# A routed feed-forward kernel: four PSUM banks for transposed rows, two for gate and up, and one piece for a unit's transposes

## The chip, the cores and the metric

The kernel runs on one core of a Trainium2 chip. Five engines work side by side, each on its own queue in order: TensorE (PE) multiplies, VectorE (DVE) and ScalarE (ACT) do elementwise work, GpSimd (POOL) issues the indirect transfers (gathers and scatters), SyncE (SP) the plain ones. PE reads from SBUF and writes to PSUM, which has eight banks of 128 x 512 fp32. The metric is the device time of one launch in microseconds. Before the change it is 3706.62 us, the median of three runs (3705.96 to 3707.15).

## The reference, cut to what matters

Tokens are 8 x 1024 = 8192 rows of 512 channels. A conditioning layer gives y; a feed-forward layer with one shared expert and 64 routed ones, eight per token, is added to x:

```python
y = clip(einsum(x * styles, weight) * dcoefs + bias, -256, 256)      # conditioning
shared = silu(y @ sh_gate_w) * (y @ sh_up_w) @ sh_down_w            # hidden 1024
topk_idx, w = route(y)                                              # 8 of 64 experts per row
g = ragged_dot(sorted_y, gate_w, group_sizes)                       # 512 -> 256, per expert
u = ragged_dot(sorted_y, up_w, group_sizes)
o = ragged_dot(silu(g) * u, down_w, group_sizes)                    # 256 -> 512
out = x + shared + zeros.at[tok].add(o * w)                         # scatter-add
```

All products are taken to fp32 accuracy: each operand is split into a high part (fp32r) and a low part, and a product is three matmuls, high x high, low x high, high x low.

## The kernel before, in words

The kernel has three stages. The conditioning runs first and writes y to memory, by rows. The shared expert follows, while the routing is worked out beside it. From about 1296 us on only the routed part is left, which is what the change touches.

The routed part works in blocks of 128 rows that go to one expert, and units of 1, 2 or 4 blocks that share one load of the expert's weights: 20 units of one block (NH), 16 of two (NP), 120 of four (NF), 532 blocks in all, with the kinds spread evenly over the sequence; unit 0 has four blocks. Further groups of units exist for other routings, behind conditions that are not met here.

For a unit, in order:

- SP loads the weights (`load`, L542): gate and up as `wg`, down as `wd`. ACT rounds them to the high parts `gh`, `dh` (`w_hi`, L560), DVE subtracts for the low parts `gl`, `dl` (`w_lo`).
- POOL gathers each block's 128 rows of y into one of 12 buffers `xg` (`gather`, L545).
- PE turns each block with four 128 x 128 transposes into one PSUM bank `pt` (`turn_x`, L549); ACT and DVE read that bank for `xh` (L552) and `xl`.
- PE makes gate and up in PSUM banks `pg`. A unit of four blocks has four products of 12 matmuls with 512 columns (`part`, L572): gate and up for the first half of the hidden channels, then for the second. ACT takes silu of the gate bank into `hf` (L716), DVE multiplies with the up bank (`mu`, L719), and `hh`, `hl` are split from `hf`. Units of two blocks do the same once, with 256 columns. A unit of one block is computed with rows on the partitions: gate and up share one bank (`half`, L581, 12 matmuls), and after silu and `mu` (L672, L673) PE turns the hidden rows (`turn_h`, L586) into the next `pg` bank, from which `hh` and `hl` are read.
- PE makes one down product per block, six matmuls with 512 columns into one of two banks `po` (`down_c`, L592); ACT weighs it into one of six buffers `oc` (L596); POOL scatters it with add into `out` (`scatter`, L599). The scatters of a unit wait for those of the unit before.

Before the change PSUM is split into two banks `pt`, four `pg` and two `po`. A block may be turned when the block two before it has been read; a gate or up result may start when the one four before it has been read.

The order of the work on each engine is fixed when the program is built. `plan` writes down a task for every step: engine, estimated duration, a lag until others see the result, a due time, and the tasks it comes after. `arrange` plays these estimates through: an engine that is free takes, of its ready tasks, the one due first. The order that comes out is the order of the queues; on the chip each instruction waits for what it really needs. Due times are set per unit from `due`, the running sum of PE's estimated work: `TURN` says how far ahead of it the transposes are due (first entry, and a step per block), `DOWN` how far behind the hidden rows the down products are. The last four units have due times of their own for the down products. Unit 0's transposes are emitted by hand during the end of the shared part.

The lines that decide the reuse of the banks:

```python
def pt_of(g):
    return pt[g % 2 if pt[1] is not None else 0]
...
add((i, "turn", s), "PE", 0.34, 0.45, t0, lambda u=u, s=s, g=g: turn_x(u, s, g), T[i, "gather", s], get(("xlo", g - 2)))
...
def wait_bank(b):
    return [bank[b - 4]] if b >= 4 else []
```

Of the kernel before, what the change touches and what calls it, by code (L numbers as in the profile page):

```python
# [15 lines left out]
ALU = mybir.AluOpType  # L16
# [50 lines left out]
def body(ctx, tc, xT, x, condT, wT, vecs, affT, rwT, ebias, wexp, shgu, shdn, cst, out):  # L67
# [32 lines left out]
    rctx, cctx = ExitStack(), ExitStack()  # L100
    FIRST = dict(xg=8, wg=2, wd=2, gh=1, gl=1, xh=1, xl=1)
    RX, ROC, RXG = 2, 6, 12
    sw = rctx.enter_context(tc.tile_pool(name="sw", bufs=1, side="right", reuse_waits="tile"))
    rp = rctx.enter_context(tc.tile_pool(name="rp", bufs=1, side="right", reuse_waits="tile"))
    yp = dctx.enter_context(tc.tile_pool(name="yp", bufs=6, reuse_waits="tile"))
# [384 lines left out]
    gh, gl, dh, dl, hh, hl = ([None] * 2 for _ in range(6))  # L490
    xh, xl = [None] * RX, [None] * RX
    hf, oc, xg = [None] * 3, [None] * ROC, [None] * RXG
    pt, po, pg = [None] * 2, [None] * 2, [None] * 4
    kinds = [
        (wg, [P, 2048], F32, "wg"), (wd, [P, 1024], F32, "wd"), (xg, [P, C], F32R, "xg"),
        (gh, [P, 2048], F32R, "gh"), (gl, [P, 2048], F32R, "gl"), (xh, [P, KC, QT], F32R, "xh"), (xl, [P, KC, QT], F32R, "xl"),
# [29 lines left out]
        return i_  # L526

    def pt_of(g):
        return pt[g % 2 if pt[1] is not None else 0]


    def load(u, a):
# [25 lines left out]
    def w_hi(u, c):  # L558
        a, sl = (gh, slice(c * 1024, (c + 1) * 1024)) if c < 2 else (dh, slice(0, 1024))
        S.copy(a[u.q][:, sl], (wg, wg, wd)[c][u.kind][:, sl])  # L560

    def w_lo(u, c):
        h_, l_, sl = (gh, gl, slice(c * 1024, (c + 1) * 1024)) if c < 2 else (dh, dl, slice(0, 1024))
        sub(l_[u.q][:, sl], (wg, wg, wd)[c][u.kind][:, sl], h_[u.q][:, sl].bitcast(F32))
# [18 lines left out]

    def turn_h(u, f, b):
        for m in range(2):
            PE.transpose(pg[b % 4][:, m * P:(m + 1) * P], hf[f % 3][:, m * P:(m + 1) * P], ident)  # L586

    def down_c(u, s, d):
        n = 0
# [23 lines left out]

    DOWN = {1: (-8.2, 1.0), 2: (6.6, 5.1), 4: (6.6, 5.1)}
    TURN = {1: (9.9, 1.0), 2: (13.2, 1.9), 4: (18.0, -1.3)}

    def plan(units):

# [2 lines left out]
        def add(key, eng, dur, lag, due, do, *after):  # L623
            t = Task(eng, dur, lag, due, do, after)
            T[key] = t
            tasks.append(t)
            return t
# [7 lines left out]
        for n, u in enumerate(units):  # L635
# [6 lines left out]
                before = [T[lw, x, 2 if a else c] for x in ("wh", "wl") for c in ((0, 1) if a == 0 else (2,))] if lw is not None else []  # L642
                add((i, "load", a), "SP", 0.1, 12.0 if a == 0 else 8.0, due - 22 + 4 * a, lambda u=u, a=a: load(u, a), *before)
            for c in range(2):
                add((i, "wh", c), "ACT", 1.08, 0.15, due - 8.3 + 2.2 * c, lambda u=u, c=c: w_hi(u, c), T[i, "load", 0], get((i - 2, "gu")))
                add((i, "wl", c), "DVE", 1.22, 0.15, due - 7.2 + 2.2 * c, lambda u=u, c=c: w_lo(u, c), T[i, "wh", c], get((i - 2, "gu")))
            xlo = []
            for s in range(u.nb):
                g = ng
                ng += 1  # L650
                t0 = due - TURN[u.nb][0] - (u.nb - 1 - s) * TURN[u.nb][1]
                gts[g] = (i, "turn", s)
                add((i, "gather", s), "POOL", 1.3, 4.5, t0 - 9, lambda u=u, s=s, g=g: gather(u, s, g), get(gts.get(g - RXG)))
                add((i, "turn", s), "PE", 0.34, 0.45, t0, lambda u=u, s=s, g=g: turn_x(u, s, g), T[i, "gather", s], get(("xlo", g - 2)))
                add((i, "xh", s), "ACT", 0.62, 0.15, t0 + 0.6, lambda u=u, s=s, g=g: x_hi(u, s, g), T[i, "turn", s], get((i - RX, "gu")))
                xlo.append(add((i, "xl", s), "DVE", 0.69, 0.15, t0 + 1.3, lambda u=u, s=s, g=g: x_lo(u, s, g), T[i, "xh", s], get((i - RX, "gu"))))
                T["xlo", g] = xlo[-1]
# [1 line left out]
            hq = [T[i - 2, "down", s] for s in range(units[n - 2].nb)] if n >= 2 else []  # L659

            def wait_bank(b):
                return [bank[b - 4]] if b >= 4 else []

            def wait_hf(f):
                return hfs.get(f - 3, [])
# [1 line left out]
            if u.nb == 1:  # L667
                b, f = nb_, nf_
                nb_, nf_ = nb_ + 2, nf_ + 1
                g0 = add((i, "gu0"), "PE", 1.37, 0.1, due, lambda u=u, b=b: half(u, 0, pg[b % 4]), *xlo, T[i, "wl", 0], T[i, "wl", 1], *wait_bank(b))  # L670
                g1 = add((i, "gu"), "PE", 1.37, 0.5, due + 1.37, lambda u=u, b=b: half(u, 1, pg[b % 4]), g0)
                si = add((i, "si"), "ACT", 0.37, 0.15, due + 3.0, lambda b=b, f=f: S.activation(hf[f % 3][:, :256], pg[b % 4][:, :256], AF.Silu), g1, *wait_hf(f))  # L672
                mu = add((i, "mu"), "DVE", 0.40, 0.15, due + 3.4, lambda b=b, f=f: V.tensor_tensor(hf[f % 3][:, :256], hf[f % 3][:, :256], pg[b % 4][:, 256:], ALU.mult), si)  # L673
                bank[b] = mu
                th = add((i, "th"), "PE", 0.3, 0.5, due + 3.9, lambda u=u, f=f, b=b: turn_h(u, f, b + 1), mu, *wait_bank(b + 1))
                o_ = lambda a, u=u: a[u.q][:, :, :P]
                p_ = lambda b=b: pg[(b + 1) % 4][:, :256].rearrange("p (m s) -> p m s", m=2)
                h_ = add((i, "hh"), "ACT", 0.37, 0.15, due + 4.6, lambda o_=o_, p_=p_: S.copy(o_(hh), p_()), th, *hq)
                l_ = add((i, "hl"), "DVE", 0.40, 0.15, due + 5.0, lambda o_=o_, p_=p_: sub(o_(hl), p_(), o_(hh).bitcast(F32)), h_, *hq)
                bank[b + 1] = l_  # L680
                hfs[f] = [th]
                lo = [l_]
                ddue = due + 5.6
            elif u.nb == 2:
                b, f = nb_, nf_
                nb_, nf_ = nb_ + 2, nf_ + 1
                prev = []
                for o in range(2):
                    for m in range(2):
                        p = add((i, "gu") if o and m else (i, "gu", o, m), "PE", 1.45, 0.5, due + 1.45 * (2 * o + m),  # L690
                                lambda u=u, o=o, m=m, b=b: part(u, o, m, pg[(b + o) % 4][:, m * 256:(m + 1) * 256]),
                                *xlo, T[i, "wl", o], *(wait_bank(b + o) if m == 0 else []), *prev)
                        prev = [p]
                    if o == 0:
                        si = add((i, "si"), "ACT", 0.61, 0.15, due + 3.2, lambda b=b, f=f: S.activation(hf[f % 3], pg[b % 4], AF.Silu), p, *wait_hf(f))
                        bank[b] = si
                mu = add((i, "mu"), "DVE", 0.69, 0.15, due + 6.1, lambda b=b, f=f: V.tensor_tensor(hf[f % 3], hf[f % 3], pg[(b + 1) % 4], ALU.mult), si, p)
                bank[b + 1] = mu
                o_ = lambda a, u=u: a[u.q][:, :, :256]
                p_ = lambda f=f: hf[f % 3].rearrange("p (m s) -> p m s", m=2)  # L700
                h_ = add((i, "hh"), "ACT", 0.61, 0.15, due + 6.9, lambda o_=o_, p_=p_: S.copy(o_(hh), p_()), mu, *hq)
                l_ = add((i, "hl"), "DVE", 0.69, 0.15, due + 7.6, lambda o_=o_, p_=p_: sub(o_(hl), p_(), o_(hh).bitcast(F32)), h_, *hq)
                hfs[f] = [l_]
                lo = [l_]
                ddue = due + 8.5
            else:
                prev = []
                for m in range(2):
                    b, f = nb_, nf_
                    nb_, nf_ = nb_ + 2, nf_ + 1  # L710
                    for o in range(2):
                        p = add((i, "gu") if o and m else (i, "gu", o, m), "PE", 2.73, 0.5, due + 2.73 * (2 * m + o),
                                lambda u=u, o=o, m=m, b=b: part(u, o, m, pg[(b + o) % 4]), *xlo, T[i, "wl", o], *wait_bank(b + o), *prev)
                        prev = [p]
                        if o == 0:
                            si = add((i, "si", m), "ACT", 0.61, 0.15, due + 5.46 * m + 3.1, lambda b=b, f=f: S.activation(hf[f % 3], pg[b % 4], AF.Silu), p, *wait_hf(f))  # L716
                            bank[b] = si
                    t0 = due + 5.46 * m + 5.8
                    mu = add((i, "mu", m), "DVE", 0.69, 0.15, t0, lambda b=b, f=f: V.tensor_tensor(hf[f % 3], hf[f % 3], pg[(b + 1) % 4], ALU.mult), si, p)  # L719
                    bank[b + 1] = mu  # L720
                    h_ = add((i, "hh", m), "ACT", 0.61, 0.15, t0 + 0.8, lambda u=u, m=m, f=f: S.copy(hh[u.q][:, m], hf[f % 3]), mu, *hq)  # L721
                    l_ = add((i, "hl", m), "DVE", 0.69, 0.15, t0 + 1.5, lambda u=u, m=m, f=f: sub(hl[u.q][:, m], hf[f % 3], hh[u.q][:, m].bitcast(F32)), h_, *hq)
                    hfs[f] = [l_]
                    lo.append(l_)
                ddue = t0 + 2.5
            for c in (2,):
                add((i, "wh", c), "ACT", 1.08, 0.15, ddue + 3.8, lambda u=u, c=c: w_hi(u, c), T[i, "load", 1], *hq)
                add((i, "wl", c), "DVE", 1.22, 0.15, ddue + 5.0, lambda u=u, c=c: w_lo(u, c), T[i, "wh", c], *hq)

            first, step_ = (2.0, 3.0) if len(units) - n <= 4 else DOWN[u.nb]  # L730
            chain = [T[units[n - 1].i, "out", s] for s in range(units[n - 1].nb)] if n else []
# [521 lines left out]
```

## Time and profile before

| | |
|---|---|
| median of three runs | 3706.62 us (3705.96 to 3707.15) |
| the profiled execution | 3707.15 us, span from first to last instruction 3705.4 us |
| granted PE clock | 0.998 |
| busy | PE 99%, POOL 56%, DVE 54%, ACT 47% |
| transposes of gathered rows (L549) | 2128 matmuls, 226.8 us busy |
| gate and up (L572) | 6528 matmuls, 2486 us busy |
| down (L592) | 3192 matmuls, 1263 us busy |
| evacuation of `pt` | xh 532 x 587 ns on ACT, xl 532 x 687 ns on DVE |

An engine's busy time counts overlapping instructions once. A PE matmul of 512 columns is shown with about 390 ns, but the next one starts before it has ended, so the distance between two starts, not the duration, is what a matmul costs. A line of the timeline reads: start in us from the beginning of the span, duration, engine, line of the program, operation, output and inputs, shapes, and how many in a row (xN); in brackets the idle time before it and what ended that. A line of the waits reads: who waited, for whom, us in total, times, longest.

### The profile page before, as it was taken

What the parts mean: (1) busy time and instruction counts of PE and PEld (TensorE: products, weight loads), DVE (VectorE), ACT (ScalarE), POOL (GpSimd) and SP (SyncE); (2) the same over time, 40 slices, a digit from 0 to 9 for tenths busy, and PEclk for the clock granted to TensorE, in tenths of its full rate; (3) what the DMA queues carried; (4) which work ended last, traced back from release to release, by engine and by line L of the source; (5) the groups of instructions that cost most, each with busy time, mean ns of one, the idle gap of its engine ahead of it and who ended that gap; (6) DMA issues with size and microseconds to landing.
All of it is one profiled execution on the core that took longest, in us unless ns stands there. A gap on an engine that the chain in (4) does not pass through costs nothing.

```text
span 3705.4 us, 49590 instructions
## 1 busy us (share of the span) xinstructions
PE 3679.9 (99%) x17819; PEld 3051.6 (82%) x17819; DVE 2009.1 (54%) x3196; ACT 1730.0 (47%) x2676; POOL 2092.1 (56%) x1597
## 2 busy tenths in 40 slices
PE   9999999999999999999999999999999999999997
PEld 7888888888888888888888888888888888888886
DVE  7765666666653355555455555455545555555553
ACT  6652111111111255555555555555556555555554
POOL 0002666666665155666666656665656656666663
PEclk9999999999999999999999999999999999999999
DMA  8852213122121377777777777777777777777664
GB/s 264 268 152 67 58 41 64 35 50 55 41 63 43 103 181 156 148 142 161 151 139 162 161 193 157 175 172 193 144 171 148 167 148 181 162 155 133 114 118 65
DMA packets 238739, 491.23 MB, mean 133 GB/s; under 512 B 43074, under 2 KB 75858, under 8 KB 230803
## 3 DMA queue, kind: packets, MB, share of 16 engines
q0 software_dynamic: 135840, 280.28, 40.4%
q1 hardware_dynamic: 101651, 206.63, 18.5%
q8 instruction: 142, 2.33, 0.3%
q10 hardware_dynamic: 992, 1.06, 0.1%
q14 instruction: 114, 0.93, 0.1%
HBM read 443.20 MB, written 195.63 MB: 172 GB/s over the span
## 4 chain that ended last, share of the span: by engine, by line
PE 98%; DVE 1%; DMA 0%; ACT 0%; POOL 0%; issue 0%; SPq 0%; POOLq 0%; DVEq 0%; ACTq 0%
PE pg L572 38%; PE po L592 20%; PE gu L124 19%; PE po L1091 9%; PE pt L549 4%; PE py L321 4%; PE pg L581 1%; PE plt L353 1%; DMA xr<-in_xT 0%; PE psm L376 0%; DMA wr<-in_wT 0%; DVE yl L72 0%; POOL out L599 0%; PE pg L586 0%; PE ps L1012 0%
## 5 line engine op out<-in xcount | busy, mean ns | idle before, releaser
L599 POOL DMA_INDIRECT out<-oc,tokw x532 | 918.8, 1727 | 664.3 <-DMA out<-oc,tokw 171.3
L572 PE MATMUL pg<-xh,gh 128*128 128x512 f32 (+1 forms) x2176 | 839.5, 386 | 0.0
L572 PE MATMUL pg<-xh,gl 128*128 128x512 f32 (+1 forms) x2176 | 824.3, 379 | 0.0
L572 PE MATMUL pg<-xl,gh 128*128 128x512 f32 (+1 forms) x2176 | 822.4, 378 | 0.0
L1061 POOL DMA_INDIRECT tab_d<-tokw,ad x512 | 567.0, 1107 | 443.2 <-DVE h L136 162.2
L545 POOL DMA_INDIRECT xg<-y_d,tokw x532 | 592.8, 1114 | 321.4 <-PE pt L549 131.0
L72 DVE TENSOR_TENSOR xl<-pt,xh 128x512 fp32r<-128x512 f32 x532 | 352.7, 687 | 406.4 <-ACT xh L552 405.6
L596 ACT ACTIVATE oc<-po,tokw 128x512 f32<-128x512 f32 x532 | 367.2, 690 | 315.6 <-PE po L592 276.0
L572 PEld LDWEIGHTS pg<-xh,gl 128*128 128x128 f32 x2176 | 409.3, 188 | 78.2
L572 PEld LDWEIGHTS pg<-xl,gh 128*128 128x128 f32 x2176 | 410.0, 188 | 71.6
L572 PEld LDWEIGHTS pg<-xh,gh 128*128 128x128 f32 x2176 | 409.1, 188 | 70.8
L719 DVE TENSOR_TENSOR hf<-hf,pg 128x512 f32<-128x512 f32 x240 | 165.0, 687 | 488.4 <-PE pg L572 488.4
L592 PE MATMUL po<-dh,hh 128*128 128x512 f32 x1064 | 428.4, 403 | 0.8 <-ACT hh L721 0.8
L592 PE MATMUL po<-dh,hl 128*128 128x512 f32 x1064 | 418.5, 393 | 0.0
L592 PE MATMUL po<-dl,hh 128*128 128x512 f32 x1064 | 415.7, 391 | 0.0
L72 DVE TENSOR_TENSOR gl<-wg,gh 128x1024 fp32r<-128x1024 f32 x312 | 376.3, 1222 | 52.0 <-ACT gh L560 51.6
L124 PE MATMUL gu<-yl,guh 128*128 128x512 f32 x1024 | 400.8, 391 | 0.2 <-DVE yl L72 0.2
L124 PE MATMUL gu<-yh,guh 128*128 128x512 f32 x1024 | 400.0, 391 | 0.1
L124 PE MATMUL gu<-yh,gul 128*128 128x512 f32 x1024 | 398.5, 389 | 0.0
L552 ACT CAST xh<-pt 128x512 fp32r<-128x512 f32 x532 | 296.7, 587 | 189.5 <-PE pt L549 134.7
L560 ACT CAST gh<-wg 128x1024 fp32r<-128x1024 f32 x312 | 324.0, 1048 | 27.4 <-PE pg L572 27.4
L716 ACT ACTIVATE hf<-pg 128x512 f32<-128x512 f32 x240 | 143.8, 599 | 295.0 <-PE pg L572 290.1
(246 smaller groups left out, 5200.0 us busy)
## 6 DMA issues: line engine op xcount, KB each, us to landing
wg<-in_wexp SPq DMA_DIRECT2D x156, 1024.0 KB
wd<-in_wexp SPq DMA_DIRECT2D x156, 512.0 KB
y_d<-yt SPq DMA_DIRECT2D x64, 256.0 KB
xn<-in_x SPq DMA_DIRECT2D x64, 256.0 KB
out<-xn SPq DMA_DIRECT2D x64, 256.0 KB
xr<-in_xT SPq DMA_DIRECT2D x60, 256.0 KB
yT_d<-yf SPq DMA_DIRECT2D x60, 256.0 KB
yr<-yT_d SPq DMA_DIRECT2D x60, 256.0 KB
```

What stands on the lines that cost most here:

```text
L72: V.tensor_tensor(o, a, b, ALU.subtract)
L124: i_ = PE.matmul(p_, lhsT=w_[:, q * KC + k], rhs=y_[k], start=n == 0, stop=n == 3 * KC - 1)
L545: queued(GP.indirect_dma_start(xg[g % RXG].bitcast(F32), None, y_d, IOA(slot_tok[:, u.block + s:u.block + s + 1], 0)))
L552: S.copy(xh[u.xq][:, :, s * P:(s + 1) * P], pt_of(g).bitcast(F32))
L560: S.copy(a[u.q][:, sl], (wg, wg, wd)[c][u.kind][:, sl])
L572: PE.matmul(out, lhsT=w_[u.q][:, c:c + P], rhs=x_[u.xq][:, k, :w], start=n == 0, stop=n == 3 * KC - 1)
L592: PE.matmul(po[d % 2], lhsT=h_[u.q][:, k, s * P:(s + 1) * P], rhs=w_[u.q][:, k * C:(k + 1) * C], start=n == 0, stop=n == 5)
L596: S.mul(oc[d % ROC], po[d % 2], slot_w[:, u.block + s:u.block + s + 1])
L599: i_ = queued(GP.indirect_dma_start(out, IOA(slot_tok[:, u.block + s:u.block + s + 1], 0), oc[d % ROC], None, compute_op=ALU.add))
L719: mu = add((i, "mu", m), "DVE", 0.69, 0.15, t0, lambda b=b, f=f: V.tensor_tensor(hf[f % 3], hf[f % 3], pg[(b + 1) % 4], ALU.mult), si, p)
L1061: i_ = GP.indirect_dma_start(places, IOA(ad, 0), tw, None)
L1091: PE.matmul(acc[j][s], lhsT=h_[:, ts], rhs=w_[c], start=c == 0 and n == 0, stop=c == HC - 1 and n == 2)
```

## The change

PSUM's split becomes four banks `pt`, two `pg`, two `po`. A block may be turned when the block four before it has been read, and a gate or up result may start when the one two before it has been read. Every unit of two or four blocks, except unit 0, gets one PE task that turns all its blocks in a row; it comes after all gathers of the unit, and after the reading of the `pt` banks that it fills. Due times of the transposes, of the down products and of the weights' casts are new numbers. Nothing changes in what is computed.

```diff
+    RPT, RPG = 4, 2
...
-    pt, po, pg = [None] * 2, [None] * 2, [None] * 4
+    pt, po, pg = [None] * RPT, [None] * 2, [None] * RPG
...
-        return pt[g % 2 if pt[1] is not None else 0]
+        return pt[g % RPT if pt[1] is not None else 0]
...
-    DOWN = {1: (-8.2, 1.0), 2: (6.6, 5.1), 4: (6.6, 5.1)}
-    TURN = {1: (9.9, 1.0), 2: (13.2, 1.9), 4: (18.0, -1.3)}
+    DOWN = {1: (-7.2, 1.0), 2: (8.4, 5.1), 4: (8.7, 6.2)}
+    TURN = {1: (12.2, 1.0), 2: (8.9, 1.3), 4: (17.7, -0.9)}
...
-                add((i, "wh", c), "ACT", 1.08, 0.15, due - 8.3 + 2.2 * c, lambda u=u, c=c: w_hi(u, c), T[i, "load", 0], get((i - 2, "gu")))
-                add((i, "wl", c), "DVE", 1.22, 0.15, due - 7.2 + 2.2 * c, lambda u=u, c=c: w_lo(u, c), T[i, "wh", c], get((i - 2, "gu")))
+                add((i, "wh", c), "ACT", 1.08, 0.15, due - 11.1 + 2.2 * c, lambda u=u, c=c: w_hi(u, c), T[i, "load", 0], get((i - 2, "gu")))
+                add((i, "wl", c), "DVE", 1.22, 0.15, due - 10.0 + 2.2 * c, lambda u=u, c=c: w_lo(u, c), T[i, "wh", c], get((i - 2, "gu")))
...
-                add((i, "gather", s), "POOL", 1.3, 4.5, t0 - 9, lambda u=u, s=s, g=g: gather(u, s, g), get(gts.get(g - RXG)))
-                add((i, "turn", s), "PE", 0.34, 0.45, t0, lambda u=u, s=s, g=g: turn_x(u, s, g), T[i, "gather", s], get(("xlo", g - 2)))
+                if not (n and u.nb > 1 and s):
+                    add((i, "gather", s), "POOL", 1.3, 4.5, t0 - 9, lambda u=u, s=s, g=g: gather(u, s, g), get(gts.get(g - RXG)))
+
+                if n == 0 or u.nb == 1:
+                    add((i, "turn", s), "PE", 0.34, 0.45, t0, lambda u=u, s=s, g=g: turn_x(u, s, g), T[i, "gather", s], get(("xlo", g - RPT)))
+                elif s == 0:
+                    for q in range(1, u.nb):
+                        gts[g + q] = (i, "turn", q)
+                        add((i, "gather", q), "POOL", 1.3, 4.5, t0 - 9 + q, lambda u=u, q=q, g=g: gather(u, q, g + q), get(gts.get(g + q - RXG)))
+                    all_ = lambda u=u, g=g: [turn_x(u, q, g + q) for q in range(u.nb)]
+                    t = add((i, "turn", 0), "PE", 0.34 * u.nb, 0.45, t0, all_, *[T[i, "gather", q] for q in range(u.nb)], *[get(("xlo", g + q - RPT)) for q in range(u.nb)])
+                    for q in range(1, u.nb):
+                        T[i, "turn", q] = t
...
             def wait_bank(b):
-                return [bank[b - 4]] if b >= 4 else []
+                return [bank[b - RPG]] if b >= RPG else []
...
-                add((i, "wh", c), "ACT", 1.08, 0.15, ddue + 3.8, lambda u=u, c=c: w_hi(u, c), T[i, "load", 1], *hq)
-                add((i, "wl", c), "DVE", 1.22, 0.15, ddue + 5.0, lambda u=u, c=c: w_lo(u, c), T[i, "wh", c], *hq)
+                add((i, "wh", c), "ACT", 1.08, 0.15, ddue + 4.7, lambda u=u, c=c: w_hi(u, c), T[i, "load", 1], *hq)
+                add((i, "wl", c), "DVE", 1.22, 0.15, ddue + 5.9, lambda u=u, c=c: w_lo(u, c), T[i, "wh", c], *hq)
```

Everywhere else `pg[b % 4]` becomes `pg[b % RPG]`.

More of the change, by code (lines that the diff above doesn't have):

```diff
@@ L585, in turn_h @@
         for m in range(2):
-            PE.transpose(pg[b % 4][:, m * P:(m + 1) * P], hf[f % 3][:, m * P:(m + 1) * P], ident)
+            PE.transpose(pg[b % RPG][:, m * P:(m + 1) * P], hf[f % 3][:, m * P:(m + 1) * P], ident)
     def down_c(u, s, d):
@@ L669, in plan @@
                 nb_, nf_ = nb_ + 2, nf_ + 1
[L670 to L673, printed above, removed]
+                g0 = add((i, "gu0"), "PE", 1.37, 0.1, due, lambda u=u, b=b: half(u, 0, pg[b % RPG]), *xlo, T[i, "wl", 0], T[i, "wl", 1], *wait_bank(b))
+                g1 = add((i, "gu"), "PE", 1.37, 0.5, due + 1.37, lambda u=u, b=b: half(u, 1, pg[b % RPG]), g0)
+                si = add((i, "si"), "ACT", 0.37, 0.15, due + 3.0, lambda b=b, f=f: S.activation(hf[f % 3][:, :256], pg[b % RPG][:, :256], AF.Silu), g1, *wait_hf(f))
+                mu = add((i, "mu"), "DVE", 0.40, 0.15, due + 3.4, lambda b=b, f=f: V.tensor_tensor(hf[f % 3][:, :256], hf[f % 3][:, :256], pg[b % RPG][:, 256:], ALU.mult), si)
                 bank[b] = mu
@@ L676, in plan @@
                 o_ = lambda a, u=u: a[u.q][:, :, :P]
-                p_ = lambda b=b: pg[(b + 1) % 4][:, :256].rearrange("p (m s) -> p m s", m=2)
+                p_ = lambda b=b: pg[(b + 1) % RPG][:, :256].rearrange("p (m s) -> p m s", m=2)
                 h_ = add((i, "hh"), "ACT", 0.37, 0.15, due + 4.6, lambda o_=o_, p_=p_: S.copy(o_(hh), p_()), th, *hq)
@@ L690, in plan @@
                         p = add((i, "gu") if o and m else (i, "gu", o, m), "PE", 1.45, 0.5, due + 1.45 * (2 * o + m),
-                                lambda u=u, o=o, m=m, b=b: part(u, o, m, pg[(b + o) % 4][:, m * 256:(m + 1) * 256]),
+                                lambda u=u, o=o, m=m, b=b: part(u, o, m, pg[(b + o) % RPG][:, m * 256:(m + 1) * 256]),
                                 *xlo, T[i, "wl", o], *(wait_bank(b + o) if m == 0 else []), *prev)
@@ L694, in plan @@
                     if o == 0:
-                        si = add((i, "si"), "ACT", 0.61, 0.15, due + 3.2, lambda b=b, f=f: S.activation(hf[f % 3], pg[b % 4], AF.Silu), p, *wait_hf(f))
+                        si = add((i, "si"), "ACT", 0.61, 0.15, due + 3.2, lambda b=b, f=f: S.activation(hf[f % 3], pg[b % RPG], AF.Silu), p, *wait_hf(f))
                         bank[b] = si
-                mu = add((i, "mu"), "DVE", 0.69, 0.15, due + 6.1, lambda b=b, f=f: V.tensor_tensor(hf[f % 3], hf[f % 3], pg[(b + 1) % 4], ALU.mult), si, p)
+                mu = add((i, "mu"), "DVE", 0.69, 0.15, due + 6.1, lambda b=b, f=f: V.tensor_tensor(hf[f % 3], hf[f % 3], pg[(b + 1) % RPG], ALU.mult), si, p)
                 bank[b + 1] = mu
@@ L712, in plan @@
                         p = add((i, "gu") if o and m else (i, "gu", o, m), "PE", 2.73, 0.5, due + 2.73 * (2 * m + o),
-                                lambda u=u, o=o, m=m, b=b: part(u, o, m, pg[(b + o) % 4]), *xlo, T[i, "wl", o], *wait_bank(b + o), *prev)
+                                lambda u=u, o=o, m=m, b=b: part(u, o, m, pg[(b + o) % RPG]), *xlo, T[i, "wl", o], *wait_bank(b + o), *prev)
                         prev = [p]
                         if o == 0:
-                            si = add((i, "si", m), "ACT", 0.61, 0.15, due + 5.46 * m + 3.1, lambda b=b, f=f: S.activation(hf[f % 3], pg[b % 4], AF.Silu), p, *wait_hf(f))
+                            si = add((i, "si", m), "ACT", 0.61, 0.15, due + 5.46 * m + 3.1, lambda b=b, f=f: S.activation(hf[f % 3], pg[b % RPG], AF.Silu), p, *wait_hf(f))
                             bank[b] = si
                     t0 = due + 5.46 * m + 5.8
-                    mu = add((i, "mu", m), "DVE", 0.69, 0.15, t0, lambda b=b, f=f: V.tensor_tensor(hf[f % 3], hf[f % 3], pg[(b + 1) % 4], ALU.mult), si, p)
+                    mu = add((i, "mu", m), "DVE", 0.69, 0.15, t0, lambda b=b, f=f: V.tensor_tensor(hf[f % 3], hf[f % 3], pg[(b + 1) % RPG], ALU.mult), si, p)
                     bank[b + 1] = mu
```

## The prediction

> **What bounds the kernel now.** I read the page first (engines, chain), then who waited for whom on PE in the routed part, then PE's timeline row by row.
>
> ```profile
> span 3705.4 us, 49590 instructions
> PE 3679.9 (99%) x17819; PEld 3051.6 (82%) x17819; DVE 2009.1 (54%) x3196; ACT 1730.0 (47%) x2676; POOL 2092.1 (56%) x1597
> PE 98%; DVE 1%; DMA 0%; ACT 0%; POOL 0%; issue 0%; SPq 0%; POOLq 0%; DVEq 0%; ACTq 0%
> ```
>
> PE is 98% of the chain that ended last. The waits of PE between 1700 and 3690 us are a single line:
>
> ```profile
> PE po L592 <- ACT hh L721: 0.8, 1, 0.8
> ```
>
> So PE waits for nothing there, and a gain can only come from PE doing its work in less time. How long that work takes is seen in the distance between starts (the durations overlap). PE's timeline, a run of 8 transposes and a run of 4:
>
> ```profile
> 2513.18 0.39 PE L572 MATMUL pg<-xh,gh 128*128 128x512 f32 x1
> 2513.41 0.39 PE L572 MATMUL pg<-xl,gh 128*128 128x512 f32 x1
> ...
> 2514.99 0.39 PE L572 MATMUL pg<-xh,gl 128*128 128x512 f32 x1
> 2515.22 0.80 PE L549 MATMUL pt<-idr,xg 128*128 128x128 f32 x8
> 2515.86 0.46 PE L572 MATMUL pg<-xh,gh 128*128 128x512 f32 x1
> 2516.16 0.39 PE L572 MATMUL pg<-xl,gh 128*128 128x512 f32 x1
> ...
> 2518.47 0.40 PE L572 MATMUL pg<-xh,gl 128*128 128x512 f32 x1
> 2518.70 0.46 PE L549 MATMUL pt<-idr,xg 128*128 128x128 f32 x4
> 2519.00 0.47 PE L592 MATMUL po<-dh,hh 128*128 128x512 f32 x1
> 2519.30 0.39 PE L592 MATMUL po<-dl,hh 128*128 128x512 f32 x1
> ```
>
> Matmuls of 512 columns start every 0.2265 us (the commonest distance of all). From 1296 us, where the shared part ends, to 3680 us no two successive starts are further apart than 0.31 us. The 0.30 us are the second start after a run of transposes: leaving a run costs something. Read off all runs: the time from the last matmul before a run to the third after it, less three ordinary distances, has the median 0.3795 us for a run of 4 and 0.7205 us for a run of 8. The difference, 0.341 us, is four transposes of 0.085 us. What is left, 0.3795 - 0.341 = 0.0385 us, is paid once per run, whatever its length.
>
> **The change, part by part.**
>
> *All transposes of a unit in one piece.* After unit 0's four blocks the routed part turns 528 more, four transposes each; the timeline has them in 236 runs of 4 transposes and 146 of 8, together 382 runs. The change makes one run per unit: 119 of 16 (units of four blocks), 16 of 8, 20 of 4, together 155. Transposes stay the same in number. Before: 236 x 0.3795 + 146 x 0.7205 = 194.8 us. After, with 0.7205 + 8 x 0.0853 = 1.403 us for a run of 16 (extrapolated: the last five distances of a run of 8 are all 0.084 to 0.086): 119 x 1.403 + 16 x 0.7205 + 20 x 0.3795 = 186.1 us. That is -8.7 us, or 227 runs fewer at 0.0385. All of it is on the path, since PE never waits. Bounds: with the medians read a thousandth of a us either way, 0.0365 to 0.0415 per run, -8.3 to -9.4 us. Matmuls 2 to 11 after a run also start 0.229 us apart against a mean of 0.228, about 0.010 us per run, after 4 as after 8. If that belongs to the run, another -2.3 us go; if it belongs to the evacuation of pt by ACT and DVE (which doesn't shrink), nothing. I take 0, because places 13 to 16 are raised more after runs of 8 than of 4, as a longer evacuation would do, and keep -2.3 as an end.
>
> *Four banks for transposed rows.* Evacuation of one unit's blocks follows its run: 4 x 0.587 us on ACT (xh), 4 x 0.687 on DVE (xl), unchanged in number, now in a burst of 2.35 and 2.75 us. Cover: ACT is 47% busy, DVE 54%, and the last xl is due some 13 us before the unit's gate matmuls (run due 15.0 us ahead). Cost 0.
>
> *Waiting for all gathers.* The run waits for four gathers at once. Taken in order of time, the k-th gather is issued 28.5 us (least) and 49 us (median) before the k-th block is turned, and lands in 3.1 / 4.4 / 9.3 us (least, median, most). The gathers that reuse the run's four xg buffers leave together instead of singly: four of some 1.1 us plus 0.3 us between, 5.6 us on POOL's queue, behind which scatters can stand. POOL is 56% busy, and the scatter behind feeds six oc buffers; it falls due before those gathers. Cost 0, lead still over 20 us.
>
> *Two banks for gate and up.* This adds the only new waits of PE. A product may start only when the one two places earlier has been read. I took the order of before, numbered its gate, up and hidden-transpose results over two banks instead of four, and compared the end of each read with the start of its bank's next writer:
>
> - results of units of four and two blocks: 509 of 510 reuses have slack, at least 1.96 us, and all but five over 3.2 us; one, at 1306 us where no down products exist yet, lacks 1.0 us. A silu ends 0.7 us after its last matmul's end, or 1.6 us when a weight cast is ahead.
> - after units of one block (20): the next unit's first product comes 0.26 us after the read in 15, 0.65 us too early in 5 (3.2 us in all); its second comes 1.36 us before hl has read the transposed hidden rows in 15 (20.3 us in all).
>
> So an unchanged order would cost 1.0 + 3.2 + 20.3 = 24.5 us. But the order is laid out anew with these waits known to it: the hidden transpose becomes ready with the same product (mu) as the next unit's first matmul and is due earlier, so it goes first; then a whole product of 2.7 us covers its reads (about 1.5 us). Down products (1.36 us each, four per unit, due up to 41 us after their unit's start now, 36 before) are at hand to fill. I take 0, near the rows of the other units; ends 0 and 24.5 us.
>
> *Due times* of casts (2.8 us earlier), dh (0.9 later), down products and runs move work inside queues that have room; the weights' loads on SP hang on those casts and move with them, 156 pairs as before, and no wait of PE names a load. The last four units keep their own down times, so the 1.2 us wait near the end and the 18 us after PE's last matmul stay, within 1.4 us (one down product) either way.
>
> Sum: -8.7 + 0 = -8.7 us. The profiled execution took 3707.15 us (span 3705.4 and 1.75 around it), 0.5 us over the median 3706.62. 3698.4 against the first is 3697.9 against the second; I say 3698.0.
>
> **The rivals.** 0.2%, about what a measurement tells from no change, is 7.4 us: under 3699.2 is faster, over 3714.0 slower.
>
> *Part of the gain is eaten* (0.21). The single-block units' five late reads stay, 3.2 us: 3701.1; with the 1.0 us at the start 3702.1. For it: the 15 good cases clear by only 0.26 us. Against: down products or transposes lie ready.
>
> *The two banks cost more than the runs give* (0.16), the slower side. Its place is the second product after each single-block unit: if the hidden transpose still comes behind the next unit's first product, PE stands 1.36 us; the full 24.5 us give 3706.6 - 8.7 + 24.5 = 3722.4. It decides from 8.7 us on, 0.44 us for each of the 20. For it: 15 of 20 stand that way today. Against: the order is made new. The Trainium skill, "Perfetto Trace Analysis", section Identifying Performance Opportunities, says that the same gap repeating on the engine that should be saturated can mean too little PSUM; by that these 20 places would show it, and the trace of before, with four banks, has none.
>
> *The clock drops in a long run* (0.02). If PE's clock halved after each run for as long as the run lasts, 1.4 us or six matmuls, 119 x 6 x 0.2265 = 162 us: 3860. Against: the granted clock is 0.998, and matmuls after runs of 8 start no further apart than after runs of 4 (0.2310, 0.2303). The Trainium skill, "TensorE: Matmul & The Clock Gate", section Part 4: PE-mode transpose, says that transposes do not count as PE-busy for the gate the same way; no run of before is long enough to test it.
>
> *The run of 16 isn't linear* (0.01 on the slow side): waits for late gathers inside it. It would take 20 us off their lead.
>
> **How the numbers follow.** Forecast 0.60, own range 3695.0 (-9.4 - 2.3) to 3699.2. Faster 0.60; same 0.21 (the eaten gain); slower 0.16 + 0.02 + 0.01 = 0.19. The range must take in the forecast and the eaten gain and may leave the slower cases out: 3695.0 to 3711.0.
>
> **What would show it.** Right: runs of 16 with about 1.40 us, 155 of them; pt's evacuation in fours; no distance over 0.31 us before the last unit; PE's waits still one line. Wrong: PE waiting for mu, a silu or hl on pg; gaps at the units of one block; distances in a run over 0.09 us; a granted clock under 0.99.

## The result and the profile after

The kernel after the change takes 3697.11 us (median of ten runs, 3696.08 to 3698.05) against 3706.40 us before (ten runs): 9.3 us less. The ratio is 0.9974, with a 95% interval from 0.9967 to 0.9982. The profiled execution took 3696.44 us, that of before 3707.15.

From the page after: the span, the engines and the chain that ended last.

```profile
span 3694.7 us, 49161 instructions
PE 3670.5 (99%) x17819; PEld 3056.7 (83%) x17819; DVE 2001.9 (54%) x3196; ACT 1734.8 (47%) x2676; POOL 2052.1 (56%) x1597
PE 99%; DVE 1%; ACT 0%; DMA 0%; issue 0%; POOL 0%; DVEq 0%; POOLq 0%; ACTq 0%
```

PE issues the same 17819 matmuls and is as full as before. What PE waited for after 1290 us (who, for whom, us in total, times, longest) is still one line:

```profile
PE po L593 <- ACT hh L733: 0.8, 1, 0.8
```

So in this profile the two banks for gate and up stop PE nowhere. The timeline of PE after shows the new run of sixteen and, a little later, the hidden transposes of a one-block unit:

```profile
2513.17 0.39 PE L573 MATMUL pg<-xh,gl 128*128 128x512 f32 x1
2513.40 1.47 PE L550 MATMUL pt<-idr,xg 128*128 128x128 f32 x16
2514.70 0.46 PE L593 MATMUL po<-dh,hh 128*128 128x512 f32 x1
2515.00 0.40 PE L593 MATMUL po<-dl,hh 128*128 128x512 f32 x1
...
2524.22 0.39 PE L593 MATMUL po<-dh,hl 128*128 128x512 f32 x1
2524.45 0.38 PE L587 MATMUL pg<-cs,hf 128*128 128x128 f32 x2
2524.59 0.48 PE L573 MATMUL pg<-xh,gh 128*128 128x512 f32 x1
2524.91 0.40 PE L573 MATMUL pg<-xl,gh 128*128 128x512 f32 x1
```

From 2513.40 to 2514.70 sixteen transposes pass, and only one late start (0.30 us, at 2515.00) follows them where before each run of four or eight had one. The two hidden transposes stand ahead of the next unit's first product, and have a late start behind them too (0.32 us). They form short runs of their own, which the prediction did not count. Why the second start behind a run comes late is not shown by any run here; what is shown is how often it is paid.

The routed part is taken from the start of the last shared down matmul to the start of PE's last matmul. These are the two lines of before, then those of after:

```profile
1296.46 0.39 PE L1091 MATMUL po<-dnh,hl 128*128 128x512 f32 x1
3686.87 0.39 PE L592 MATMUL po<-dh,hl 128*128 128x512 f32 x1
1295.95 0.39 PE L1103 MATMUL po<-dnh,hl 128*128 128x512 f32 x1
3677.39 0.39 PE L593 MATMUL po<-dh,hl 128*128 128x512 f32 x1
```

It took 2390.4 us before and takes 2381.4 us after, -9.0 us. The two profiled executions differ by 10.7 us: that of before is the slowest of its ten runs, that of after lies 0.7 us under its median. The other 1.7 us lie ahead of the routed part (0.5) and behind it (1.2). A second profile of after gives 2381.4 us again, so the routed part repeats better than the time as a whole; of before there is one profile. The runs are counted in PE's timeline, and each is priced as the prediction does it:

| between full matmuls | before | after |
|---|---|---|
| runs of gathered rows | 382 (236 of 4, 146 of 8) | 155 (119 of 16, 16 of 8, 20 of 4) |
| hidden transposes in a run of their own | 5 (15 more joined to a run of 4) | 20 |
| all runs | 387 | 175 |
| time of all runs | 198.7 us | 190.4 us |

The runs account for -8.3 us. This takes 0.1195 us as the ordinary distance behind a matmul of 256 columns, beside which 32 runs of before stand and none of after; with half of 0.2265 us instead, before has 199.1 us and the runs account for -8.7. The other -0.3 to -0.7 us lies in the ordinary matmuls, which I can't assign further.

### The profile page after: what moved, and what is told of

It reads as the page before. It is cut to its first block, busy times and chain, and to the rows that moved or that the text cites. A ratio compares the mean times of both kernels' runs of the same rounds, so it can differ in the third digit from the quotient of the medians.

```text
span 3694.7 us, 49161 instructions
## 1 busy us (share of the span) xinstructions
PE 3670.5 (99%) x17819; PEld 3056.7 (83%) x17819; DVE 2001.9 (54%) x3196; ACT 1734.8 (47%) x2676; POOL 2052.1 (56%) x1597
## 4 chain that ended last, share of the span: by engine, by line
PE 99%; DVE 1%; ACT 0%; DMA 0%; issue 0%; POOL 0%; DVEq 0%; POOLq 0%; ACTq 0%
PE pg L573 38%; PE po L593 20%; PE gu L125 19%; PE po L1103 10%; PE pt L550 5%; PE py L322 4%; PE pg L582 1%; PE plt L354 1%; PE psm L377 0%; DVE yl L72 0%; PE pg L587 0%; PE ps L1024 0%; DMA cd<-in_condT 0%; DVE yt L366 0%; PE ps L263 0%; PE psm L280 0%
## 5 line engine op out<-in xcount | busy, mean ns | idle before, releaser
L600 POOL DMA_INDIRECT out<-oc,tokw x532 | 897.4, 1687 | 682.0 <-ACT oc L597 270.8
L573 PE MATMUL pg<-xh,gh 128*128 128x512 f32 (+1 forms) x2176 | 829.1, 381 | 0.0
L546 POOL DMA_INDIRECT xg<-y_d,tokw x532 | 576.0, 1083 | 332.7 <-issue 101.5
L72 DVE TENSOR_TENSOR xl<-pt,xh 128x512 fp32r<-128x512 f32 x532 | 337.7, 684 | 165.4 <-ACT xh L553 164.1
L72 DVE TENSOR_TENSOR hl<-hf,hh 128x512 fp32r<-128x512 f32 x256 | 175.5, 691 | 269.7 <-ACT hh L733 269.7
L553 ACT CAST xh<-pt 128x512 fp32r<-128x512 f32 x532 | 281.8, 595 | 78.9 <-PE pt L550 74.2
```

What stands on the lines that cost most here:

```text
L72: V.tensor_tensor(o, a, b, ALU.subtract)
L546: queued(GP.indirect_dma_start(xg[g % RXG].bitcast(F32), None, y_d, IOA(slot_tok[:, u.block + s:u.block + s + 1], 0)))
L553: S.copy(xh[u.xq][:, :, s * P:(s + 1) * P], pt_of(g).bitcast(F32))
L573: PE.matmul(out, lhsT=w_[u.q][:, c:c + P], rhs=x_[u.xq][:, k, :w], start=n == 0, stop=n == 3 * KC - 1)
L600: i_ = queued(GP.indirect_dma_start(out, IOA(slot_tok[:, u.block + s:u.block + s + 1], 0), oc[d % ROC], None, compute_op=ALU.add))
```

## The experiments

Three theories stood against each other: the time goes by the *number of runs* on PE (entering and leaving one costs about 0.04 us); the gain comes from the *new due times*; it comes from the *banks*, or the banks cost something that the rest pays for. Each group of kernels stands against runs of before on its own chip: 3706.21 us for the first four, 3706.18 for the next four, 3706.51 for the last three. The difference in the last column is taken against these; before's medians in all groups lie between 3706.18 and 3706.51 us. The 95% interval of one comparison reaches about 0.1% (3 to 4 us) to each side. So by their time alone after, old due times, blind and thrice differ from before, while apart (0.9983 to 1.0001), pairs, new due times, two pg banks and single (1.0000 to 1.0018) are not clear of it; there the routed part and the counts carry the argument, each from one profile.

| kernel | runs of gathered rows + hidden alone | routed part, us | time, us | against its own before |
|---|---|---|---|---|
| before | 382 + 5 | 2390.4 | 3706.40 | |
| after | 155 + 20 | 2381.4 | 3697.11 | -9.3 |
| blocks apart | 321 + 2 | 2387.2 | 3703.49 | -2.7 |
| pairs in before | 274 + 15 | 2388.3 | 3705.93 | -0.3 |
| after, old due times | 155 + 1 | 2380.2 | 3696.05 | -10.2 |
| before, new due times | 333 + 19 | 2387.9 | 3705.27 | -0.9 |
| two pg banks alone | 373 + 16 | 2392.0 | 3706.89 | +0.7 |
| plan blind to the reads | 155 + 20 | 2409.4 | 3724.68 | +18.5 |
| each transpose thrice | 155 + 20 | 2740.0 | 4058.24 | +352.1 |
| single blocks in before | 462 + 20 | 2393.6 | 3709.51 | +3.3 |

### Blocks apart: the piece undone

```diff
-                if not (n and u.nb > 1 and s):
+                if True:
...
-                if n == 0 or u.nb == 1:
+                if True:
```

> After, but every block is a PE task of its own again (four pt banks, two pg banks and the new due times stay). The order then has 321 runs of transposes after unit 0 where before has 382 and after 155. If the time goes by the number of runs (0.0385 us each): 61 runs fewer than before, -2.3 us against before, so it gives back 6.4 us of the gain of 9.3. If the gain came from the banks or from the due times: about -9 us against before, as after.

3703.49 us (3702.25 to 3704.44). With all banks and due times of after, the gain falls from 9.3 to 2.7 us; its fastest run is 3.7 us over the slowest run of after (3698.58). The routed part is 3.2 us shorter than before's, which goes with the 64 runs that it has fewer. What makes the gain is the piece.

### Pairs in one piece, in the kernel before

```diff
+                elif s % 2 == 0:
...
+                    two = lambda u=u, s=s, g=g: [turn_x(u, s + q, g + q) for q in range(2)]
+                    t = add((i, "turn", s), "PE", 0.68, 0.45, t0, two, T[i, "gather", s], T[i, "gather", s + 1], get(("xlo", g - 2)), get(("xlo", g - 1)))
```

> Before (two pt banks, four pg banks, old due times), but two blocks of a unit are one PE task: 274 runs, 254 of 8 and 20 of 4. By the number of runs: 108 fewer than before, -4.2 us. If the gain of after needs its banks or due times: 0 against before.

3705.93 us, but spread from 3703.13 to 3707.29: three of eleven runs lie under 3703.9, eight over 3705.6. The profile belongs to the lower ones (span 3701.9). PE's waits in it:

```profile
PE pg L572 <- ACT xh L552: 1.2, 1, 1.2
PE po L592 <- ACT hh L729: 0.8, 1, 0.8
PE pg L572 <- DVE xl L72: 0.3, 1, 0.3
```

```profile
3658.32 0.79 PE L549 MATMUL pt<-idr,xg 128*128 128x128 f32 x8
3660.27 0.50 PE L572 MATMUL pg<-xh,gh 128*128 128x512 f32 x1 [1.16 <-ACT xh L552]
3661.10 0.50 PE L572 MATMUL pg<-xl,gh 128*128 128x512 f32 x1 [0.33 <-DVE xl L72]
```

Near the end, at 3659 us, a product waits for the rows that have just been turned to be read into xh and xl; the two distances are 1.41 and 0.84 us where 0.23 is usual, 1.8 us lost. Routed part -2.1 us, and -3.9 without that loss, against -4.2 expected. By its median (-0.3 us) the kernel missed that forecast and came out as the other theory has it, by which the gain needs the banks or due times of after; only this one profile, less its loss, speaks for the runs. What the slower eight runs lose in addition is not in it and stays open. One sign is on record: seven of the eight list a granted clock of 0.997, the three lower ones 0.998. In before's runs both values occur at low and at high times; but the blind plan's profile below has a stretch of 3.4 us at half the clock behind the same kind of wait. One such stretch lowers the mean clock of 3706 us by 0.0005, from the 0.9977 of this profile to what is listed as 0.997. It would cost some 1.6 us of the 2.6 between the levels; that the slower runs have it is not shown.

### After with the old due times

```diff
-    DOWN = {1: (-7.2, 1.0), 2: (8.4, 5.1), 4: (8.7, 6.2)}
-    TURN = {1: (12.2, 1.0), 2: (8.9, 1.3), 4: (17.7, -0.9)}
+    DOWN = {1: (-8.2, 1.0), 2: (6.6, 5.1), 4: (6.6, 5.1)}
+    TURN = {1: (9.9, 1.0), 2: (13.2, 1.9), 4: (18.0, -1.3)}
```

(and the casts' dues as before)

> After with all due times of before: 155 runs as in after. By the number of runs -8.7 us against before, as after. If the new due times make the gain, or hide the waits of the two pg banks: near 0 or slower than before.

3696.05 us (3695.55 to 3696.64): the whole gain is there without the new numbers, and about 1 us more. PE's waits are the one line of after. The due times neither make the gain nor hide a wait. The extra microsecond is taken up below.

### Before with the new due times

```diff
-    DOWN = {1: (-8.2, 1.0), 2: (6.6, 5.1), 4: (6.6, 5.1)}
-    TURN = {1: (9.9, 1.0), 2: (13.2, 1.9), 4: (18.0, -1.3)}
+    DOWN = {1: (-7.2, 1.0), 2: (8.4, 5.1), 4: (8.7, 6.2)}
+    TURN = {1: (12.2, 1.0), 2: (8.9, 1.3), 4: (17.7, -0.9)}
```

> Before with all due times of after and nothing else: 333 runs. By the number of runs: 49 fewer, -1.9 us against before. If the due times make the gain: about -9 us.

3705.27 us (3704.72 to 3706.6), -0.9 us; the routed part is 2.5 us shorter in its profile, and the stretch behind PE's last start 0.7 us longer (19.2 us against 18.5). The new numbers do little, and what they do goes with the 49 runs that they happen to join.

### Two pg banks alone

```diff
-    RPT, RPG = 4, 2
+    RPT, RPG = 2, 2
...
-    DOWN = {1: (-7.2, 1.0), 2: (8.4, 5.1), 4: (8.7, 6.2)}
-    TURN = {1: (12.2, 1.0), 2: (8.9, 1.3), 4: (17.7, -0.9)}
+    DOWN = {1: (-8.2, 1.0), 2: (6.6, 5.1), 4: (6.6, 5.1)}
+    TURN = {1: (9.9, 1.0), 2: (13.2, 1.9), 4: (18.0, -1.3)}
...
-                if not (n and u.nb > 1 and s):
+                if True:
...
-                if n == 0 or u.nb == 1:
+                if True:
```

(written from after, with the casts' dues as before; it comes to before with `pg[b % 2]` and `bank[b - 2]`, and its lines are numbered as in after)

> Before with two pg banks instead of four and nothing else (two pt banks, blocks as tasks of their own, old due times; two banks stay unused): 373 runs. If the planned order hides the waits of two banks: -0.3 us by the number of runs, no wait of PE on pg in the trace. If two banks cost what the order of before suggests: up to +24.5 us, most of it behind the 20 units of one block.

3706.89 us (3705.59 to 3708.4), 0.7 us over before, with a 95% interval of the ratio from 0.9992 to 1.0010: no difference is shown. PE's waits, in a profile of the slowest run (3708.4 us):

```profile
PE pt L550 <- DVE xl L72: 1.4, 1, 1.4
PE po L593 <- ACT hh L733: 0.8, 1, 0.8
```

There is one new wait, up to 1313.9 us at the start of the routed part, for a pt bank and not for a pg one; it is the size of the whole difference and more. Nothing repeats. Two banks for gate and up are free here, as long as the plan knows of them.

### The plan blind to the reads

```diff
-                g1 = add((i, "gu"), "PE", 1.37, 0.5, due + 1.37, lambda u=u, b=b: half(u, 1, pg[b % RPG]), g0)
+                g1 = add((i, "gu"), "PE", 1.37, -1.3, due + 1.37, lambda u=u, b=b: half(u, 1, pg[b % RPG]), g0)
...
-                th = add((i, "th"), "PE", 0.3, 0.5, due + 3.9, lambda u=u, f=f, b=b: turn_h(u, f, b + 1), mu, *wait_bank(b + 1))
+                th = add((i, "th"), "PE", 1.3, -1.29, due - 34.0, lambda u=u, f=f, b=b: turn_h(u, f, b + 1), mu, *wait_bank(b + 1))
...
+                ahead, lag = (40.0, 0.0) if n and units[n - 1].nb == 1 else (0.0, 0.5)
```

(silu, multiply, `hh` and `hl` of these units: 0.01 us, no lag; the next unit's products are due 40 us earlier)

> After, but the plan is told that in a unit of one block the reads of pg (silu, multiply, hh, hl) take next to no time, and that the unit behind it comes first; so the hidden transpose stands behind the next unit's first product and directly ahead of the second, in 19 of 20 units, much as in the order of before. Same work, same 155 runs. If the plan's knowledge of the waits is what makes two banks free: PE waits some 1.3 to 1.5 us for hl at each place, +25 to +30 us against after (about 3724). If two banks never bind: as after.

3724.68 us (3724.22 to 3725.33), 27.6 us over after. The same work with the same runs; PE's waits, and one of the twenty places in its timeline:

```profile
PE pg L573 <- DVE hl L72: 18.4, 20, 0.9
PE pg L573 <- ACT xh L553: 1.3, 1, 1.3
PE pg L573 <- DVE hf L685: 1.0, 1, 1.0
PE po L593 <- ACT hh L734: 0.8, 1, 0.8
PE pg L573 <- DVE xl L72: 0.2, 1, 0.2
```

```profile
2535.18 0.38 PE L587 MATMUL pg<-cs,hf 128*128 128x128 f32 x2
2536.48 0.50 PE L573 MATMUL pg<-xh,gh 128*128 128x512 f32 x1 [0.92 <-DVE hl L72]
2536.82 0.40 PE L573 MATMUL pg<-xl,gh 128*128 128x512 f32 x1
2536.00 0.42 DVE L72 TENSOR_TENSOR hl<-pg,hh 128x256 fp32r<-128x256 f32 x1 [0.97 <-ACT hh L690]
```

The hidden transposes stand behind the next unit's first product, and its second waits until DVE has read the bank (the last line: hl ends at 2536.42). The run of two costs 1.42 us instead of 0.24, 20 times: 23.7 of the 28.0 us that the routed part grew. Three single gaps near the end, at 3658.6, 3679.5 and 3680.2 us, take 3.1 us beyond the usual distance. Behind the last two come matmuls that start 0.427 us apart:

```profile
3681.94 0.63 PE L573 MATMUL pg<-xl,gh 128*128 128x512 f32 x1
3682.36 0.63 PE L573 MATMUL pg<-xh,gl 128*128 128x512 f32 x1
3682.79 0.63 PE L573 MATMUL pg<-xh,gh 128*128 128x512 f32 x1
```

The granted clock is 0.50 there, the third figure from the end of this line (a stretch of the span, its length, the busy time of each engine, the clock, the share of DMA, GB/s):

```profile
3681.40:3684.80 3.40, 3.40 (x10) 2.67 (x9) 1.89 (x2) 0.93 (x2) 1.51 (x1) 0.50 0.09 16
```

This stretch costs some 1.6 us. No other profile has it in its routed part, and that the waits bring it on is not shown. The gaps and this stretch are no cost of the 20 places. The repeating gap is the slower rival of the prediction, with its place and its price. The Trainium skill ("Perfetto Trace Analysis", Identifying Performance Opportunities) says that the same gap repeating on the engine that should be saturated can mean too little PSUM; the 20 gaps look like this, but after has the same two banks and none of them. It differs only in the order.

### Each transpose three times

```diff
-        for k in range(KC):
+        for k in [k for k in range(KC) for _ in range(3)]:
```

> After, but each transpose is made three times into the same place (same output): runs of 48 instead of 16, of some 4.1 us. If transposes in a run cost 0.0853 us each at any length and the number of runs is unchanged: 2 x 2128 x 0.0853 = +363 us, about 4060, distances in the run 0.085, granted clock 0.998. If the clock gate does not count transposes as work: the clock falls in or after runs of over 3.4 us, distances of 0.17 and 0.45 us show, and the time is far beyond 4100.

4058.24 us (4057.28 to 4059.36): 361.1 us over after, 363 were expected. The clock, and a run in PE's timeline:

```profile
core 0: 4055.6 us, clock 0.998
```

```profile
2505.58 0.39 PE L573 MATMUL pg<-xh,gl 128*128 128x512 f32 x1
2505.81 4.15 PE L550 MATMUL pt<-idr,xg 128*128 128x128 f32 x48
2509.80 0.46 PE L573 MATMUL pg<-xh,gh 128*128 128x512 f32 x1
2510.10 0.40 PE L573 MATMUL pg<-xl,gh 128*128 128x512 f32 x1
```

By their medians the distances in the run are 0.083 to 0.086 us from the third to the last, and the second start behind it comes after 0.30 us, as after a run of four. So the cost of leaving a run does not depend on its length, and the clock does not fall. The Trainium skill ("TensorE: Matmul & The Clock Gate", Part 4: PE-mode transpose) says that transposes do not count as busy the same way; runs of 4.1 us between matmuls show no sign of it here, and the measurement decides.

### Single blocks in the kernel before

```diff
-            t = min((t for t in open_[e] if t.ready <= t0), key=lambda t: t.due)
+            t = min((t for t in open_[e] if t.ready <= t0), key=lambda t: (turned and t.turn, t.due))
+            if e == "PE":
+                turned = t.turn
```

(`t.turn` marks the transposes of gathered rows)

> Before, but the plan never puts two blocks in a row while anything else is ready on PE: 462 runs instead of 382. By the number of runs +3.1 us against before (3709.3). If runs as such don't matter: 0.

3709.51 us (3708.78 to 3710.87), +3.3 us. More runs, more time, with no wait added: PE's waits are the one line of before. By its time alone it is not clear of before (1.0000 to 1.0018). Between this kernel and after lie 482 - 175 = 307 runs and 2393.6 - 2381.4 = 12.2 us of the routed part, 0.040 us per run; on that line the kernel before should take 2389.8 us and took 2390.4, blocks apart 2387.3 and 2387.2, before with new due times 2388.4 and 2387.9.

### Where the extra microsecond comes from

With the old due times, 19 of the 20 hidden transposes follow a run of sixteen directly. Three kernels on one chip: after again; the old due times with such joining preferred; the old due times with it avoided.

```diff
+            t.turn = t.eng == "PE" and (t.dur == 0.3 or t.lag == 0.45)
...
-            t = min((t for t in open_[e] if t.ready <= t0), key=lambda t: t.due)
+            t = min((t for t in open_[e] if t.ready <= t0), key=lambda t: (not (turned and t.turn), t.due))
+            if e == "PE":
+                turned = t.turn
```

(this is the joined kernel; the split one marks hidden transposes 1 and gathered rows 2, and its key begins with `bool(turned and t.turn and turned != t.turn)`)

> After, unchanged, as the measure for the two others on the same chip: 3697.1, 175 runs counting the 20 short ones of the hidden transposes.

> After with all due times of before, and on PE a transposing task follows another transposing task if one is ready: 155 runs of gathered rows as in after, but 20 of them take in the two hidden transposes of a one-block unit, which after turns in 20 short runs of their own. In the run with the old due times a run of 16 and 2 together took 1.574 us, apart 1.399 + 0.237. If joining runs is all: 20 x 0.062 = -1.2 us against after (3695.9). If the old due times had another merit, more; if neither, as after.

> After with all due times of before, but a hidden transpose is never put next to a run of gathered rows while anything else is ready: 175 runs again, as after. If joining was the whole advantage of the old due times: as after (3697.1). If the old due times themselves are better: 3696.

After again 3697.12 us (3696.69 to 3698.58), joined 3696.12 (3695.59 to 3696.58), split 3697.31 (3696.65 to 3698.59). Routed parts 2381.4, 2380.2 and 2381.2 us. A joined place in PE's timeline:

```profile
2522.88 1.47 PE L550 MATMUL pt<-idr,xg 128*128 128x128 f32 x16
2524.18 0.41 PE L587 MATMUL pg<-cs,hf 128*128 128x128 f32 x2
2524.34 0.48 PE L573 MATMUL pg<-xh,gh 128*128 128x512 f32 x1
2524.66 0.39 PE L573 MATMUL pg<-xl,gh 128*128 128x512 f32 x1
```

One late start instead of two: 1.573 us together, 1.400 + 0.237 apart. The joined kernel is 1.0 us under after and 10.4 under before, and each of its runs is faster than each of the two others'; the split one comes out as after. The old due times have no merit but this, and the kernel with them (3696.05 us) is as fast as the joined one.

## Why the prediction was right

It gave 3698.0 us with a range from 3695.0 to 3711.0 and faster as the likeliest; 3697.11 was measured.

The mechanism held: fewer runs at a fixed price each, on an engine that waits for next to nothing. That the number came within 0.9 us is partly luck, since small terms that the sum left out, of 0.3 to 0.7 us each and of both signs, nearly cancel.

- *PE bounds the routed part and waits for nothing.* Right, before and after: one wait of 0.8 us in both.
- *0.0385 us per run.* Right in kind, a little small: the experiments give 0.040 over 307 runs. A run of 16 took 1.399 us, 1.403 were extrapolated; 155 runs came as counted.
- *-8.7 us from 227 runs fewer.* All runs together, hidden transposes included, gave -8.3 to -8.7. What the sum left out: 15 pairs of hidden transposes stood ahead of a run before, at 0.216 us each, and all 20 are apart after, at 0.237, which costs 0.3 us. What it had as an end, up to 2.3 us from calmer matmuls behind runs, can be at most the 0.7 us that lie outside the runs; no experiment isolates it. The bounds of the price, 0.0365 to 0.0415, were read unevenly: a thousandth of a us on each median gives 0.0355 at the lower end.
- *Two banks: 0, between 0 and 24.5 us.* Right at the lower end: two banks alone change nothing that repeats. The upper end had a real mechanism: with the hidden transposes of all 20 one-block units behind the next unit's first product, 23.7 us were lost at these places, 1.18 each, where 20.3 had been read off for 15, 1.36 each. The whole loss of 28.0 us is not the same sum as the forecast's 24.5. What decides between them was named: hidden transposes ahead of the next unit's first product. In after, that product starts 1.7 to 2.3 us after mu has been read, and 2.3 us or more remain between the end of hl's read and the second product.
- *Gathers.* Right that they cost nothing, PE waits for none. In order of time the k-th gather leads the k-th turned block by at least 29.7 us from 1313 us on. Five blocks ahead of that have 17.6 to 22.3 us, two of them less than the 20 forecast; before, two blocks at 1315 and 1319 us have 24.2 and 27.5, less than the 28.5 that was read as the least.
- *Due times: nothing.* Right for the new numbers as such; both experiments on them move the time only through the runs that they join or part.
- *The clock.* The rival with a chance of 0.02 is answered by runs of 4.1 us. Single distances in a run of 16 reach 0.093 us, over the 0.09 that was to show it wrong; those in before's runs of 8 do so too.
- *No distance over 0.31 us.* Nearly: before the wait near the end the largest in after is 0.32 us, behind hidden transposes. Before has the same (0.32 us at 2453.9 us), which the prediction read as 0.31.
- *pt's evacuation in fours.* In part: DVE reads four blocks in a row 101 times, ACT 52 times and mostly two and two (146 times). It costs PE no wait.
- *The end.* The distance at the wait near the end stayed at 1.2 us. The stretch behind PE's last start was 18.5 us before and 17.3 after in the two profiles, but 17.9 in another profile of after, so it is no part of the gain.

## What to carry to other kernels

When PE is full, look at the distances between starts and not at durations: here each run of small matmuls between wide ones had a price that the busy time hides, and joining runs was worth the count times that price, no more. A result buffer could be halved here because the order of work is made with its waits known to it, and the trace of before told beforehand where it would bind: compare the end of each read with the next writer in the smaller ring. Changes made together should be taken apart: here one of three parts made the gain (the piece), one allowed it (the banks: a piece of four blocks fills four), and one cost a microsecond (the due times).

## What I had not expected

Two transposes of another kind, fp32 from the hidden rows, join a run of gathered rows when they follow it: 0.17 us more (1.573 - 1.400) instead of 0.24 on their own. When they come ahead of the run it is 0.22 (0.595 - 0.379, the 15 places of before, a run of four); behind a run of four it is 0.18 (18 places of blocks apart). So the order within the joined run decides most of what joining saves. A run of 48 transposes keeps the pace of 0.085 us to its end and costs no more to leave than one of four (0.30 us to the second start behind it). And the pairs in before came out at two levels some 2.6 us apart, of which the profile shows only the lower.
